# Attention in blocks of two steps: scores of both, then the other TensorE work, then values of both, with PSUM shared out for it

## The chip, the cores and the metric

The kernel runs on one core of one Trainium2 chip. The metric is the device time of one execution in microseconds. Before the change it is 6248.07 us, the median of three runs (6247.93 to 6248.6).

## The reference, cut to what matters

The input is x, four images of 128 channels and 64 by 64 points, all in float32. Layer 0 is softmax attention over the 4096 points of an image, with four heads of 32 channels:

```python
attn = jax.nn.softmax(jnp.einsum('bhnd,bhmd->bhnm', Q, K) * scale, axis=-1)
out = jnp.einsum('bhnm,bhmd->bhnd', attn, V)
...
y = out @ Wo + bo + x_flat          # then a layer norm over the channels
```

Layer 1 adds three things computed from the output of layer 0: a 3x3 convolution, a mixing of channels in the frequency plane (in the kernel two Hilbert and channel matmuls and a flipped addition), and a selective scan ("mamba") along the 4096 points:

```python
xs = silu(conv1d(xi));  dt = softplus(dt_proj(x_dbl))
h  = exp(dt * A) * h + dt * B * xs  # 256 channels x 16 states
y  = (C . h + xs * D) * silu(z);  ym = y @ out_proj
return spatial + spectral + ym
```

## The kernel before, in words

**Units of work.** The 4096 points of an image are cut into chunks of 512 (32 chunks in all). A *half* H is one chunk of queries with one pair of heads; there are 64. A half takes 32 *steps*, one for each tile of 128 keys, so there are 2048 steps. The main loop (lines 984 to 1023) counts steps with `t`; one pass of it writes the instructions of one step[...].

**One step of attention.** `scores_for_exp` (line 470) computes the scores of 128 keys against 512 queries for two heads: six matmuls (query, low part of the query, minus the maximum), each on 64 of the 128 rows of TensorE, into two PSUM banks; ScalarE turns them into `e = exp(s)` in SBUF (line 486). `scores_for_max` (line 422) computes scores for the half that comes next: four matmuls of the same 64-row kind, whose maximum VectorE takes (line 441, the tile `part`). `times_values` (line 489) multiplies e with the values: two matmuls with 33 output columns each, into PSUM tile `po`, which a whole half accumulates. The values of a step are written one step later, behind the scores of the next. So TensorE does: scores of t, values of t-1, scores of t+1, values of t, and so on. At the end of a half, ScalarE and VectorE copy `po` to `oz` (lines 507 and 508).

**All other work is in jobs.** Projections, transposes, the convolution, the gates and so on are generators (`project_q`, `maxima`, `sigmoid`, `convolve`, ...). A job yields a string of letters that says what it needs next: P a place for a TensorE piece, A for ScalarE, D for VectorE, B a PSUM bank. `Plan.step` (line 122) is called once in a step, after the scores and ahead of the values, and goes over the jobs by rank and due time (`plan.at`, lines 955 to 981). While attention runs, odd steps offer two places each of P, A and D; even steps offer one place of A only. So other TensorE work comes at most once in two steps, between scores and values.

**The scan.** Each chunk has two halves of the channels with 16 states each, so 32 *states* `v`. One state takes `scan_decay` (ScalarE, `dA = exp(dt*A)` into PSUM, line 780), `scan_input_term` (GpSimd, `db`, line 785) and `scan_state` (VectorE scan, line 793; GpSimd times C and sum, lines 796 to 812). One state is done in two steps. The scan of chunk c starts `LAG` = 2 x 64 + 16 steps behind the attention of chunk c, so when attention has ended, 144 steps of scan are left. In the last two chunks the sum over states is done on TensorE (line 806).

**PSUM.** [...] `s1` (two, scores for the maximum), `s2` (two, scores for exp), `o` (one, values), `dA` (one), `m0` and `m1` (one each, for all the jobs, given out by the plan and released some steps later).

Of the kernel before, what the change touches and what calls it, by code (L numbers as in the profile page):

```python
# [9 lines left out]
F32 = mybir.dt.float32  # L10
# [71 lines left out]
class Job:  # L82
# [4 lines left out]
    def __init__(self, gen):  # L87
        self.gen = gen
        self.done = False
        self.need = None  # L90
        self.advance(None)

    def advance(self, bank):
        try:
            self.need = self.gen.send(bank)
        except StopIteration:
            self.done = True


class Plan:  # L100


    def __init__(self, banks, buffers):
        self.t = None
        self.places = buffers
        self.seq = 0
        self.later = []
        self.jobs = []
        self.free = list(range(banks))
        self.freed = []  # L110

    def at(self, t, rank, gen):
        self.seq += 1
        self.later.append((t, rank, self.seq, gen))

    def now(self, rank, gen):
        self.at(self.t, rank, gen)

    def release(self, bank, steps=1):
        self.freed.append((self.t + steps, bank))  # L120

    def step(self, t, places):

        self.t = t
        self.places |= places
        self.free += [bank for when, bank in self.freed if when <= t]
        self.freed = [e for e in self.freed if e[0] > t]
        for e in sorted((e for e in self.later if e[0] <= t), key=lambda e: e[:3]):
            self.jobs.append((e[1], e[0], e[2], Job(e[3])))
            self.later.remove(e)  # L130
        self.jobs = sorted((j for j in self.jobs if not j[3].done), key=lambda j: j[:3])
        kept = 0
        for *_, job in self.jobs:
            bank = None
            if "B" in job.need and len(self.free) <= kept:
                continue
            if any(c != "B" and not self.places[c] for c in job.need):
                kept += "B" in job.need
                continue
            for c in job.need:  # L140
                if c == "B":
                    bank = self.free.pop(0)
                else:
                    self.places[c] -= 1
            job.advance(bank)
            while not job.done and job.need == "P" and self.places["P"]:
                self.places["P"] -= 1
                job.advance(None)
        self.jobs = [j for j in self.jobs if not j[3].done]

# [5 lines left out]
def attention_then_conv_mamba(  # L156
# [114 lines left out]
    def constants_of_attention():  # L271
        yield ""
# [3 lines left out]
    def constants_of_the_rest():  # L276


        yield ""
# [11 lines left out]
        yield ""  # L291
# [4 lines left out]
        yield ""  # L296
        nc.vector.tensor_scalar(negA, negA, -1.0, None, ALU.mult)


        bank = yield "PB"  # L300
        pb = bank_tile(bank, [P, 1], "pb")
        for k in range(PAIRS):
            nc.tensor.matmul(pb, Wo[k], bvk[:, k : k + 1], start=k == 0, stop=k == PAIRS - 1)
        yield "D"
        plan.release(bank, 2)
# [19 lines left out]
    plan = Plan(2, {"x": 2, "f": 1})  # L325

    def bank_tile(bank, shape, name):
        return psum.tile(shape, F32, tag=f"m{bank}", name=name)
# [10 lines left out]
    def project_kv(b, i):  # L339
# [5 lines left out]
        yield ""  # L345
        bank = yield "PB"
        pk = bank_tile(bank, [P, L], f"pk_{nm}")
        nc.tensor.matmul(pk, Wk, xk, start=True, stop=True)
        yield "DA"
        plan.release(bank, 2)  # L350
        hi = att.tile([P, L], F32R, tag="khi", name=f"khi_{nm}")
        lo = att.tile([P, L], F32R, tag="klo", name=f"klo_{nm}")
        nc.scalar.activation(hi, pk, AF.Identity, bias=bk)
        nc.vector.scalar_tensor_tensor(lo, pk, bk, hi, ALU.add, ALU.subtract)
# [4 lines left out]
        bank = yield "PB"  # L359
        pv = bank_tile(bank, [P, TPC, HEADS, HD], f"pv_{nm}")  # L360
# [8 lines left out]
        plan.places["x"] += 1  # L369
        yield "A"  # L370
        plan.release(bank)
        vst = att.tile([P, TPC, HEADS, HD + 1], F32, tag="vst", name=f"vst_{nm}", bufs=1)
# [30 lines left out]
    def project_q(H):  # L403
# [4 lines left out]
        bank = yield "PB"  # L408
        pq = bank_tile(bank, [P, L], f"pq_{H}")
        nc.tensor.matmul(pq, Wq[k], xqs[c], start=True, stop=True)  # L410
        yield "DA"
        plan.release(bank, 2)
        q = att.tile([P, 2, L], F32R, tag="Q", name=f"Q_{H}", bufs=3)
        bias = bq[:, k : k + 1]
        nc.scalar.activation(q[:, 1, :], pq, AF.Identity, bias=bias)
        nc.vector.scalar_tensor_tensor(q[:, 0, :], pq, bias, q[:, 1, :], ALU.add, ALU.subtract)
# [5 lines left out]
    def scores_for_max(H, s):  # L422
# [6 lines left out]

        tag = "s2" if H == 0 and s % 2 else "s1"  # L430
# [12 lines left out]
    def maxima(H):  # L443

        bank = yield "B"
# [8 lines left out]
        yield ""  # L454
        pm = bank_tile(bank, [P, L], f"pm_{H}")
# [4 lines left out]
        yield ""  # L460
        plan.release(bank, 2)
        mhi = att.tile([P, L], F32R, tag="th", name=f"mhi_{H}", bufs=1)
        mm = att.tile([P, L], F32R, tag="MX", name=f"MX_{H}")
        nc.scalar.activation(mhi, pm, AF.Copy, scale=-1.0)
        nc.vector.scalar_tensor_tensor(mm, mhi, minus_lo, pm, ALU.mult, ALU.subtract)
# [4 lines left out]
    def scores_for_exp(H, m):  # L470
# [4 lines left out]
        s = psum.tile([P, 2, L], F32, tag="s2", name=f"s2_{H}_{m}")  # L475
# [9 lines left out]
        e = att.tile([P, 2, L], F32, tag="e", name=f"e_{H}_{m}", bufs=3)  # L485
# [24 lines left out]
    def normalise(H, t0):  # L510
# [10 lines left out]
        yield ""  # L521
# [8 lines left out]
        yield ""  # L530
        nc.gpsimd.tensor_tensor(oz[k], oz[k], r, ALU.mult)  # L531
        if k == PAIRS - 1:
            plan.at(t0, 0, output_projection(H // PAIRS))
# [7 lines left out]
    def output_projection(c):  # L541
# [5 lines left out]
        bank = yield "PB"  # L547
        py = bank_tile(bank, [P, TPC, P], f"py_{c}")
        for t in range(TPC):
            if t == TPC // 2:  # L550
                yield "P"
            ts = slice(t * P, (t + 1) * P)
            for k in range(PAIRS):
                nc.tensor.matmul(py[:, t, :], oz[k][:, ts], Wo[k], start=k == 0, stop=False)  # L554
            nc.tensor.matmul(py[:, t, :], xr[:, ts], ident, start=False, stop=True)
# [5 lines left out]
        for t in range(TPC):  # L561
            nc.vector.bn_stats(st[:, t, :], py[:, t, :])
# [6 lines left out]
        yield ""  # L569
        nc.scalar.activation(q, v, AF.Ln)  # L570
        nc.scalar.activation(r, q, AF.Exp, scale=-0.5)
        yield ""
# [5 lines left out]
        yield ""  # L578
        yield "D"
        plan.release(bank, 2)  # L580

        xh = loc.tile([P, TPC, P], F32, tag="xh", name=f"xh_{c}", bufs=2)
        XH[c] = xh
        for t in range(TPC):
            nc.vector.tensor_scalar(
                xh[:, t, :],
                py[:, t, :],
# [9 lines left out]
    def sigmoid(z, tag, nm):  # L597
# [6 lines left out]
        bank = yield "AB"  # L604
        ln = bank_tile(bank, [P, L], f"ln_{nm}")
        nc.scalar.activation(ln, a, AF.Ln, bias=ones)
        yield "D"
        plan.release(bank, 2)
# [10 lines left out]
    def mamba_input(c):  # L619
# [14 lines left out]
        bank = yield "PB"  # L634
        pt = bank_tile(bank, [P, TPC, P], f"pt_{c}")
        for t in range(TPC):
            nc.tensor.transpose(pt[:, t, :], XH[c][:, t, :], ident)
        yield "A"
        plan.release(bank)
# [19 lines left out]
    def scan_input(c, hf):  # L659

        bank = yield "PB"
        pi = bank_tile(bank, [P, RPC, W], f"pi_{c}_{hf}")
        nc.tensor.matmul(pi, inw[:, hf * P : (hf + 1) * P], inner(c), start=True, stop=True)  # L663
        yield "A"
        plan.release(bank)
        xi = loc.tile([P, L + TAPS - 1], F32, tag=f"sg{hf}", name=f"xi_{c}_{hf}", bufs=1)
        nc.scalar.activation(xi[:, : TAPS - 1], carry[:, hf, :], AF.Copy)
        nc.scalar.activation(xi[:, TAPS - 1 :], pi.rearrange("p r w -> p (r w)"), AF.Identity)
        nc.scalar.activation(carry[:, hf, :], xi[:, L:], AF.Copy)
        s = loc.tile([P, L], F32, tag=f"xs{hf}", name=f"xs_{c}_{hf}", bufs=1)  # L670
        bank = yield "DB"
        ps = bank_tile(bank, [P, L], f"conv_{c}_{hf}")
# [13 lines left out]
        plan.release(bank, 2)  # L686
# [7 lines left out]
    def scan_bc(c):  # L694

        bank = yield "PB"
        pd = bank_tile(bank, [DTR + 2 * NS, L], f"pd_{c}")
        for hf in range(NH):
            nc.tensor.matmul(pd, xpw[:, hf, :], xss[c][hf], start=hf == 0, stop=hf == NH - 1)  # L699
        yield "A"  # L700
        plan.release(bank)
# [8 lines left out]
    def scan_dt(c, hf, xd):  # L710
        bank = yield "PB"
        pdt = bank_tile(bank, [P, L], f"pdt_{c}_{hf}")
# [5 lines left out]
        yield "A"  # L718
        plan.release(bank)
# [11 lines left out]
        bank = yield "AB"  # L731
        ln = bank_tile(bank, [P, L], f"lnw_{c}_{hf}")
        nc.scalar.activation(ln, w, AF.Ln)
        yield "DA"
        plan.release(bank, 2)
# [364 lines left out]
```

## Time and profile before

| | |
|---|---|
| median of three runs | 6248.07 us |
| the profiled execution: its own time | 6247.33 us |
| its span, first to last instruction | 6245.5 us |
| matmul rows on TensorE | 32076, busy 6001.6 us (96%) |
| busy: VectorE, ScalarE, GpSimd | 4284.2 us (69%), 3582.9 us (57%), 4605.3 us (74%) |
| first and last exp of the attention (line 486) | start at 130.7 and 5967.6 us |
| last scan of a state (line 793) | starts at 6230.6 us |
| granted TensorE clock, mean | 0.978 |

A float32 matmul appears as two rows (two passes). Rows of matmuls that run side by side on different parts of the array start a few ns apart. Their ends are modelled, and so this document works with the distance from one start to the next. In the timeline the columns are start, length, engine, line, operation, output <- inputs, shape and count, and in square brackets the idle time ahead of it and what ended it. Neighbouring equal rows are merged, "x4" being four of them; then the length runs from the first start to the last end.

### The profile page before, as it was taken

How to read it: one execution, taken by the hardware profiler on the slowest of the kernel's cores; microseconds unless marked ns; L12 is line 12 of the kernel's file. 1: busy time of each engine (PE TensorE's matmuls, PEld its weight loads, DVE VectorE, ACT ScalarE, POOL GpSimd, SP SyncE). 2: the span in 40 equal slices, each digit the busy share in tenths (PEclk: the TensorE clock that was granted, in tenths of full speed). 3: DMA queues.
4: the chain of work that ended last, by engine and by line, in shares of the span. 5: the costliest groups of instructions: out<-in, count | busy, mean ns of one | idle time of the engine just before them, and what ended most of it. 6: DMA issues, size and time to landing. Idle time of an engine off the chain costs nothing.

```text
span 6245.5 us, 83489 instructions
## 1 busy us (share of the span) xinstructions
PE 6001.6 (96%) x32076; PEld 2540.6 (41%) x32076; DVE 4284.2 (69%) x4405; ACT 3582.9 (57%) x4858; POOL 4605.3 (74%) x4951
## 2 busy tenths in 40 slices
PE   5999999999999999999999999999999999999956
PEld 2444444444444444444444444444444444444321
DVE  4556777777777677777767777767776766677556
ACT  1455666665666656566665556656565655665642
POOL 0006887777888777888887788877788877778866
PEclk7999999999999999999999999999999999999976
DMA  3002222223222222223232222222322222212223
GB/s 111 14 15 60 62 58 58 65 65 103 72 75 58 62 62 63 59 65 84 76 87 62 65 62 65 55 60 70 98 70 63 57 52 56 56 53 55 59 68 93
DMA packets 234225, 404.98 MB, mean 65 GB/s; under 512 B 38872, under 2 KB 40416, under 8 KB 233824
## 3 DMA queue, kind: packets, MB, share of 16 engines
q1 hardware_dynamic: 229440, 397.75, 23.3%
q8 instruction: 251, 4.11, 0.3%
q10 hardware_dynamic: 4384, 1.89, 0.1%
q14 instruction: 150, 1.23, 0.1%
HBM read 350.54 MB, written 49.02 MB: 64 GB/s over the span
## 4 chain that ended last, share of the span: by engine, by line
PE 80%; POOL 9%; DVE 5%; ACT 3%; issue 2%; DMA 1%; ACTq 0%; SPq 0%; POOLq 0%; DVEq 0%
PE po L498 27%; PE s L478 25%; PE s L434 13%; PE pf L857 4%; POOL hs L797 3%; DVE part L441 2%; ACT e L486 2%; DVE hs L793 2%; POOL db L785 1%; PE pi L663 1%; PE pdt L713 1%; POOL acc L812 1%; PE pq L410 1%; PE pd L699 1%; PE py L554 1%
## 5 line engine op out<-in xcount | busy, mean ns | idle before, releaser
L441 DVE TENSOR_REDUCE part<-s 128x2 f32<-128x1024 f32 x2048 | 2501.0, 1222 | 1613.6 <-PE s L434 1611.9
L486 ACT ACTIVATE e<-s 128x1024 f32<-128x1024 f32 x2048 | 2094.1, 1023 | 2257.5 <-PE s L478 2249.3
L498 PE MATMUL po<-e,V 128*33 128x512 f32 x8192 | 2160.1, 605 | 2.8 <-DVE oz L508 0.3
L478 PE MATMUL s<-Q,K 64*128 64x512 f32 x8192 | 1500.7, 444 | 25.3 <-ACT e L486 20.2
L793 DVE TENSOR_TENSOR_SCAN hs<-dA,state,db 128x512 f32<-128x512 f32 x1024 | 1305.7, 1275 | 158.9 <-ACT dA L780 69.2
L797 POOL TENSOR_TENSOR hs<-hs,bc 128x512 f32<-128x512 f32 x1024 | 1307.0, 1276 | 82.0
L434 PE MATMUL s<-K,Q 64*128 64x512 f32 x8192 | 1297.7, 395 | 44.4 <-DVE part L441 42.0
L478 PEld LDWEIGHTS s<-Q,K 64*128 64x128 f32 x8192 | 611.5, 185 | 1753.7 <-ACT e L486 1186.1
L785 POOL TENSOR_TENSOR db<-u,bc 128x512 f32<-128x512 f32 x954 | 1223.0, 1282 | 1.6 <-DMA bc<-bcd 1.6
L812 POOL TENSOR_TENSOR acc<-acc,hs 128x512 f32<-128x512 f32 x900 | 1151.7, 1280 | 70.6
L796 POOL COPY state<-hs 128x1 f32<-128x1 f32 x1024 | 212.6, 208 | 976.6 <-DVE hs L793 976.1
L434 PEld LDWEIGHTS s<-K,Q 64*128 64x128 f32 x8192 | 763.7, 186 | 280.5 <-DVE part L441 102.9
L478 PE MATMUL s<-MX,sel 64*128 64x512 f32 x4096 | 810.3, 392 | 0.0
L780 ACT ACTIVATE dA<-dt,negA 128x512 f32<-128x512 f32 x1024 | 702.5, 686 | 146.8 <-DVE hs L793 146.7
L498 PEld LDWEIGHTS po<-e,V 128*33 128x33 f32 x8192 | 299.2, 109 | 899.0 <-issue 865.0
L478 PEld LDWEIGHTS s<-MX,sel 64*128 64x128 f32 x4096 | 383.8, 184 | 90.0
L857 PE MATMUL pf<-xp,cw 128*128 128x512 f32 x576 | 288.2, 617 | 0.0
L450 POOL COPY wide<-mx 128x128 f32<-128x128 f32 x256 | 63.2, 292 | 196.9 <-DVE mx L447 196.9
L806 PE MATMUL acc<-hs,cst 128*128 128x512 f32 x128 | 110.8, 969 | 86.7 <-POOL hs L797 86.7
L531 POOL TENSOR_TENSOR oz<-oz,rz 128x512 f32<-128x512 f32 x64 | 81.9, 1279 | 106.7 <-DMA rz<-rd 106.7
L857 PEld LDWEIGHTS pf<-xp,cw 128*128 128x128 f32 x576 | 96.1, 188 | 131.9 <-issue 126.9
L554 PE MATMUL py<-wat_vo,oz 128*128 128x128 f32 x512 | 83.0, 285 | 22.6 <-POOL oz L531 18.6
(134 smaller groups left out, 3561.0 us busy)
## 6 DMA issues: line engine op xcount, KB each, us to landing
bc<-bcd SPq DMA_DIRECT2D x512, 512.0 KB
K<-kd SPq DMA_DIRECT2D x64, 256.0 KB
rz<-rd SPq DMA_DIRECT2D x128, 128.0 KB
vd<-vst SPq DMA_DIRECT2D x32, 264.0 KB
V<-vd SPq DMA_DIRECT2D x32, 264.0 KB
xq<-in_x SPq DMA_DIRECT2D x32, 256.0 KB
xk<-in_x SPq DMA_DIRECT2D x32, 256.0 KB
kd<-khi SPq DMA_DIRECT2D x32, 256.0 KB
```

The source lines that it names most:

```text
L434: nc.tensor.matmul(sc[:, j, :], QT[H][rows[j], n, t * P : (t + 1) * P], KK[k][m][rows[j], :], start=n == 0, stop=n == 1,)
L441: nc.vector.tensor_reduce(part[H][:, t, :, m], sc, AX.X, ALU.max)
L478: nc.tensor.matmul(s[:, j, :], sel[rows[j], :] if n == 2 else KK[k][i][rows[j], t * P : (t + 1) * P], mov[rows[j], :], start=n == 0, stop= ...
L486: nc.scalar.activation(e, s, AF.Exp)
L498: nc.tensor.matmul(po[H][used[j], :], VA[i][:, t, 2 * k + j, :], e[:, j, :], start=m == 0, stop=m == NT - 1,)
L780: nc.scalar.activation(dA[c, v], dts[c][hf], AF.Exp, scale=negA[:, k : k + 1])
L785: engine.tensor_tensor(db[c, v], us[c][hf], bcs[c, n][:, 0, :], ALU.mult)
L793: nc.vector.tensor_tensor_scan(hs, dA.pop((c, v)), db.pop((c, v)), state[:, k : k + 1], ALU.mult, ALU.add)
L796: nc.gpsimd.tensor_copy(state[:, k : k + 1], hs[:, L - 1 :])
L797: nc.gpsimd.tensor_tensor(hs, hs, bcs[c, n][:, 1, :], ALU.mult)
L812: nc.gpsimd.tensor_tensor(accs[c, hf], accs[c, hf], hs, ALU.add)
L857: nc.tensor.matmul(pf, cw[:, k, :], xps[c][:, dy : dy + RPC, dx : dx + W], start=k == 0, stop=False)
```

## The change

The loop now counts *blocks* `u` of two steps (a half has UH = 16, a chunk SLOT = 32 blocks, attention UNITS = 1024). TensorE's order in a block is: scores for the maximum of step 2u, scores for exp of 2u and of 2u+1, scores for the maximum of 2u+1, the jobs' work, values of 2u and of 2u+1. The values no longer lag by a step.

PSUM: `sA` (two banks) takes both scores for the maximum; `sB` (two banks) takes the scores for exp of 2u and then, in the same block, the jobs' temporary tiles (T); `sC` (two banks) takes the scores for exp of 2u+1 and then dA; `m` (one bank, need M) takes the sums that last over blocks (convolution and conv1d); `o` is as before. A job that takes a temporary tile must evacuate it in the same block: its need names all at once (`PTA`: matmul, tile and ScalarE place), and the VectorE operations that read such a tile are in a phase of their own ("g", need G), written after the scan of the block. D-jobs come in a first phase between the two maxima. `bn` now reads a copy in SBUF that ScalarE makes; the output projection is done in two parts in two blocks; the convolution does one matmul (C) in a block. The places in a block are P 2, C 1, T 2, A 3, D 2, E 1, G 1. LAG becomes 64 blocks (128 steps), LEAD 8 steps, e has two buffers in place of three, and bc is loaded for state pair n+2, at even v.

```diff
-    def step(self, t, places):
...
+    def begin(self, u, places):
+        self.u = u
+        self.places = dict(places)
+        self.temps = []
+        self.buffers["M"] += sum(when <= u for when in self.freed)
+        self.freed = [when for when in self.freed if when > u]
+
+    def phase(self, kinds):
...
         for *_, job in self.jobs:
...
+            while not job.done and self.may(job, kinds):
+                bank = None
+                for c in job.need:
+                    if c == "T":
+                        if not self.temps:
+                            self.temps = self.temporary(u)
+                        bank = self.temps.pop(0)
+                    elif c == "M":
+                        bank = self.lasting(u)
+                    if c in self.buffers:
+                        self.buffers[c] -= 1
+                    elif c != "g":
+                        self.places[c] -= 1
+                job.advance(bank, u)
         self.jobs = [j for j in self.jobs if not j[3].done]
+
+    def may(self, job, kinds):
+        if not job.need:
+            return "" in kinds and self.u > job.u
+        if any(c not in kinds for c in job.need):
+            return False
+        left = self.places | self.buffers | {"g": 9}
+        return all(left[c] >= job.need.count(c) for c in job.need)
...
-    def bank_tile(bank, shape, name):
-        return psum.tile(shape, F32, tag=f"m{bank}", name=name)
+    def temporary(u):
+
+        t = psum.tile([P, 2, L], F32, tag="sB", name=f"tmp_{u}")
+        return [t[:, 0, :], t[:, 1, :]]
+
+    def lasting(u):
+        return psum.tile([P, L], F32, tag="m", name=f"sum_{u}")
...
@@ def project_q(H):
-        bank = yield "PB"
-        pq = bank_tile(bank, [P, L], f"pq_{H}")
+        pq = yield "PTAG"
         nc.tensor.matmul(pq, Wq[k], xqs[c], start=True, stop=True)
-        yield "DA"
-        plan.release(bank, 2)
...
         nc.scalar.activation(q[:, 1, :], pq, AF.Identity, bias=bias)
+        yield "g"
         nc.vector.scalar_tensor_tensor(q[:, 0, :], pq, bias, q[:, 1, :], ALU.add, ALU.subtract)
...
@@ def sigmoid(z, tag, nm):
         nc.scalar.activation(a, a, AF.Exp, scale=-1.0)
-        bank = yield "AB"
-        ln = bank_tile(bank, [P, L], f"ln_{nm}")
+        ln = yield "ATG"
         nc.scalar.activation(ln, a, AF.Ln, bias=ones)
-        yield "D"
-        plan.release(bank, 2)
+        yield "g"
         nc.vector.scalar_tensor_tensor(a, z, 0.0, ln, ALU.min, ALU.subtract)
...
@@ def scores_for_exp(H, m, tag):
-        e = att.tile([P, 2, L], F32, tag="e", name=f"e_{H}_{m}", bufs=3)
+        e = att.tile([P, 2, L], F32, tag="e", name=f"e_{H}_{m}", bufs=2)
...
@@ def output_projection(c):
+        xh = loc.tile([P, TPC, P], F32, tag="xh", name=f"xh_{c}", bufs=2)
+        for t0 in range(0, TPC, 2):
+            bank = yield "PPTA"
+            py = bank[:, : 2 * P].rearrange("p (t c) -> p t c", t=2)
...
+            nc.scalar.activation(xh[:, t0 : t0 + 2, :], py, AF.Identity)
...
@@ def scan_decay(c, v):
-        tag = "o" if plan.t >= HALVES * NT + 2 and v % 2 else "dA"
-        dA[c, v] = psum.tile([P, L], F32, tag=tag, name=f"dA_{c}_{k}")
+        if plan.u > UNITS and v % 2:
+            dA[c, v] = psum.tile([P, L], F32, tag="o", name=f"dA_{c}_{k}")
+        else:
+            dA[c, v] = psum.tile([P, 2, L], F32, tag="sC", name=f"dA_{c}_{k}")[:, 0, :]
...
@@ def convolve(c):
         for k in range(9):
             if k:
-                yield "P"
+                yield "PC"
...
+    def maxima_of(t):
+        h, s = divmod(t + LEAD, NT)
+        if 0 <= h + 1 < HALVES:
+
+            scores_for_max(h + 1, s, "sC" if h < 0 and s % 2 else "sA")
+
+    places = {"P": 2, "C": 1, "T": 2, "A": 3, "D": 2, "E": 1, "G": 1}
+    most = {"P": 4, "C": 4, "T": 2, "A": 4, "D": 4, "E": 4, "G": 4}
+    u = 3 - SLOT
     end = (CHUNKS + 3) * SLOT
...
+    while u < end or not plan.idle():
+        busy = -LEAD // 2 <= u < UNITS
+        plan.begin(u, places if busy else most)
+        H, m = divmod(2 * u, NT)
+        v = u - LAG
+        scan = 0 <= v < CHUNKS * STATES
+        maxima_of(2 * u)
+        plan.phase(["D", "M"])
         if 0 <= H < HALVES:
+            scores_for_exp(H, m, "sB")
+            scores_for_exp(H, m + 1, "sC")
+        maxima_of(2 * u + 1)
+        if scan:
+            scan_decay(*divmod(v, STATES))
+
+        n = v // NH + 2
+        if v % NH == 0 and 0 <= n < CHUNKS * NS:
+            scan_load(*divmod(n, NS))
+        plan.phase(["P", "C", "T", "A", "E", "G", "M", "x", "f", ""])
+        if scan:
+            scan_state(*divmod(v, STATES))
+        if 0 <= v + 2 < CHUNKS * STATES:
+            late = u > UNITS
+            scan_input_term(*divmod(v + 2, STATES), nc.vector if late else nc.gpsimd)
+        plan.phase(["g"])
+        if 0 <= H < HALVES:
             times_values(H, m)
+            times_values(H, m + 1)
+        u += 1
```

Jobs are handled alike throughout: the other projections (`project_kv`, `scan_input`, `scan_bc`, `scan_dt`, `gate`, `spectral`, `mamba_input`) trade `PB` ... `A`/`D` for `PTA` or `PPTA`, and `scan_dt` takes its logarithm with `AATG`. The due times of the jobs are halved, from steps to blocks, some with small shifts (the gates at block 5 of a chunk, mamba input at 8, the convolution at 19).

## The prediction

> **What bounds the kernel now.** I read the busy shares first, then the chain of work that ended last, then the costliest groups.
>
> ```profile
> PE 6001.6 (96%) x32076; PEld 2540.6 (41%) x32076; DVE 4284.2 (69%) x4405; ACT 3582.9 (57%) x4858; POOL 4605.3 (74%) x4951
> PE 80%; POOL 9%; DVE 5%; ACT 3%; issue 2%; DMA 1%; ACTq 0%; SPq 0%; POOLq 0%; DVEq 0%
> L441 DVE TENSOR_REDUCE part<-s 128x2 f32<-128x1024 f32 x2048 | 2501.0, 1222 | 1613.6 <-PE s L434 1611.9
> L609 DVE SCALAR_TENSOR_TENSOR sg_x<-xs,ln_x 128x512 f32<-128x512 f32 x64 | 43.3, 676 | 3.1 <-ACT ln_x L606 3.1
> PE s L434 <- DVE part L441: 42.0, 81, 1.3
> PE s L478 <- ACT e L486: 20.2, 25, 1.5
> ```
>
> TensorE is on 80% of the chain, and VectorE and ScalarE mostly idle for TensorE's scores. TensorE itself waits for them only 42.0 + 20.2 us. But 96% is modelled; how full it is shows in the distances between starts. One step without other work, in the timeline of all engines around 5420 us:
>
> ```profile
> 5419.60 0.73 PE L478 MATMUL s<-Q,K 64*128 64x512 f32 x4
> 5420.18 0.39 PE L478 MATMUL s<-MX,sel 64*128 64x512 f32 x2
> 5420.41 0.62 PE L434 MATMUL s<-K,Q 64*128 64x512 f32 x4
> 5420.67 1.02 ACT L486 ACTIVATE e<-s 128x1024 f32<-128x1024 f32 x1 [0.80 <-PE s L478]
> 5420.95 1.05 PE L498 MATMUL po<-e,V 128*33 128x512 f32 x4
> 5421.07 1.23 DVE L441 TENSOR_REDUCE part<-s 128x2 f32<-128x1024 f32 x1
> 5421.59 0.69 ACT L780 ACTIVATE dA<-dt,negA 128x512 f32<-128x512 f32 x1
> 5421.94 0.73 PE L478 MATMUL s<-Q,K 64*128 64x512 f32 x4
> 5422.20 1.11 ACT L733 ACTIVATE lnw<-u 128x512 f32<-128x512 f32 x2
> ```
>
> Rows run in pairs (two heads side by side). The MX pair takes 5420.41 - 5420.18 = 0.23. The first two pairs take 0.58, so the first takes 0.35, which is 0.12 too much. The two K,Q pairs take 0.54 up to the first value, 0.08 more than 0.46. The values (two passes) take 0.99. A pass of 512 columns takes 0.43, from the timeline of the tail, where 16 of them run without a break, (7.03 - 0.59)/15:
>
> ```profile
> 6049.77 7.03 PE L857 MATMUL pf<-xp,cw 128*128 128x512 f32 x16
> ```
>
> So 0.13 of the 0.99 is not work. **Each round of scores and values loses 0.12 + 0.08 + 0.13 = 0.33 us** in a step of 2.34. What a real wait looks like, in the timeline at 532 us:
>
> ```profile
> 530.98 1.22 DVE L441 TENSOR_REDUCE part<-s 128x2 f32<-128x1024 f32 x1
> ...
> 532.25 0.73 PE L434 MATMUL s<-K,Q 64*128 64x512 f32 x4
> ...
> 532.92 0.15 PEld L498 LDWEIGHTS po<-e,V 128*33 128x33 f32 x4 [0.37 <-issue]
> ```
>
> The reduction ends at 532.20, TensorE goes on 0.05 later, and its two pairs then take 0.67 instead of 0.54: a wait costs its length plus some 0.12.
>
> [...]
>
> **The change, part by part** (1024 blocks; times from the block's start on TensorE).
>
> *One round less.* Today a block of two steps has two rounds, with or without jobs between them; then it has one: -0.33 x 1024 = **-338 us**. A block without jobs falls from 4.68 to 4.35. The jobs' matmuls stay; by the planner's rules I count 21 of 32 blocks per chunk with TensorE jobs, and the trace before has 20.7 (613 of 949 pairs of steps from 500 to 5960 us), so this is nothing.
>
> *Both maxima in sA.* The first one's second pair starts at 0.35; VectorE begins 0.43 later (5420.64 to 5421.07), takes 1.23, and release takes 0.05: free at 2.06. TensorE arrives after six exp pairs, 0.35 + 7 x 0.23 = 1.96. It waits 0.10 and reloads for 0.12, in every block: **+225 us**. Bounds: 0.10 (loads slip ahead of the wait, +102) to 0.35 (VectorE 0.13 late, +358). Behind the waiting matmuls stand the whole of the jobs and the values. Today s1 has a full step, and the same release is free.
>
> *Values in the same block.* The last pair of the first exp scores starts at 1.04, its e at +0.49 = 1.53 (5420.18 to 5420.67), until 2.55. Without jobs the values arrive at 2.06 + 0.35 + 0.23 + 0.08 = 2.72: no wait. The second e starts 2.45 (ScalarE starts the next some 0.10 before the end: 5421.59 against 5421.69), ends 3.47; its values come at 2.72 + 0.89 = 3.61. **0**, and covered by 0.1 us only. Two buffers of e suffice for the same reason.
>
> *Jobs' tiles in sB, read by VectorE behind the scan.* In a block with one 512-column job TensorE needs 0.12 + 0.86 + 0.10 more, and everybody is done in time. The exposed ones are logarithms in blocks without TensorE work. From the due times and places, these are blocks 6 and 10 of a chunk (gate) and 15 and 17 (scan input). ScalarE there: second e 2.45, dA 3.37, jobs from 3.98 (dA to lnw 0.61). In 15, 17 abs, exp, ln are 0.62 + 0.62 + 0.68: 5.90; in 6 xr (0.61), exp and ln give the same; in 10 exp and ln 5.28, but the scan (dA ends 4.06, + 0.05 + 1.27) holds VectorE until 5.38. Then 0.68 (row L609) and twice 0.05 of release: sB free at 6.68, 6.68, 6.68 and 6.11. TensorE wants it for the next exp at 4.57 + 0.58 = 5.15. With the reload: 1.65 three times and 1.08, less 0.22 each, since the next sA wait vanishes behind it: 5.2 us per chunk. For 31 chunks of scan input and 30 of gates **+157 us** (bounds: 0, if other matmuls fall into these blocks, to 300, if pq, pm and lnw are exposed as well).
>
> *End of a half.* oz on ScalarE, then VectorE (0.59 + 0.69, rows L507, L508) now stand ahead of the next maximum: 0.4 on average x 64 = **+26** (0 to 45).
>
> *Today's waits* (62 us, with 106 reloads of 0.12) belong to the order that goes: **-75** (0 to -90).
>
> *Small.* Output projection in two parts, [...] its ScalarE copies (some 0.45 each, half of a 128x512 row) lie beside 1.3 us of TensorE work; bn and xh push the second reduction, +3. DMAs: bc, loaded later by its place, waits for the same GpSimd product as today and still has two blocks; zd, zc and rd keep their distance on SP: 0.
>
> *Tail.* LAG leaves 64 states behind the attention instead of 72. The first ones there take 3.17 each, GpSimd bound:
>
> ```profile
> 5984.19 1.28 DVE L793 TENSOR_TENSOR_SCAN hs<-dA,state,db 128x512 f32<-128x512 f32 x1 [3.37 <-POOL acc L812]
> 5987.36 1.28 DVE L793 TENSOR_TENSOR_SCAN hs<-dA,state,db 128x512 f32<-128x512 f32 x1 [1.16 <-POOL acc L812]
> ```
>
> 8 x 3.2 = 26, and a little for jobs put ahead of the sum on TensorE: **-28** (0, if the last chunk's own chain sets the end, to -45).
>
> Sum: -338 + 225 + 157 + 26 - 75 + 10 - 28 = -23. From the profiled execution's 6247.3 that is 6224; the median of the runs is 0.7 higher: **6225 us**. The gain is real and mostly handed back at PSUM.
>
> **Rivals.** (1) *Forecast*: most comes back through sA and sB; own range 6150 to 6300. Chance 0.45. (2) *sB is covered*: the logarithms fall beside matmuls or the scan is early; the 157 go: 6225 - 157 = 6068, say 6070. For it: 21 of 32 blocks have cover. Against: A 3 and rank leave those four blocks to ScalarE alone. Chance 0.20. (3) *VectorE becomes the bound, slower.* Place: a block without jobs. Its second reduction starts at 2.41 + 0.43 = 2.84, ends 4.07; the scan waits for dA, 4.11 to 5.38; the next first reduction is due at 4.57 + 0.78 = 5.35. The slack is nil where today the scan has a bank of its own and nobody on TensorE behind it. From there each delay of the scan (db from GpSimd, busy 74%; a job's operation ahead of it) goes straight into sA, and beyond 0.4 into sC too. If the scan is 0.5 late in the 11 blocks without jobs of each of 30 chunks: +165, so 6390. Against: GpSimd prepares db two states ahead. Chance 0.35. That the rounds don't fall to one is excluded by the order in which the loop writes.
>
> **Numbers.** 0.2% (12.5 us) is about what a measurement of this kernel can tell from no change. Faster: all of (2) and just over half of (1), 0.45. Same: 0.10. Slower: (3) and the rest of (1), 0.45. The range takes in the middle of (2) and of (3): 6075 to 6390, leaving a tenth on each side.
>
> **What would show it.** Right: score runs of ten pairs with one change per block; in each block TensorE idle before L434 for VectorE (part) by 0.1, about 1000 times; idle before exp scores for VectorE (sg_x, sg_z) by 1 to 1.6, about 120 times; a tail some 28 us shorter. Wrong: the first wait is absent or far over 0.1; sB waits also for Q, MX and dt, or for none; TensorE idle for scan tiles in sC. A result under 6100 refutes the sB term, one over 6350 the claim that VectorE keeps up.

## The result, and the profile after

The changed kernel takes **6486.22 us** (median of four runs, 6482.18 to 6490.97), the kernel before 6248.00 beside it. The ratio is 1.038, with a 95% interval from 1.036 to 1.040: 238 us slower. The forecast was 6225, and its range ended at 6390. The profiled execution took 6482.18 us with a span of 6480.4, against 6224 forecast for it: 258 us are to be explained.

First the busy shares and the chain of work that ended last, after the change:

```profile
PE 5923.2 (91%) x32076; PEld 2624.0 (40%) x32076; DVE 4457.2 (69%) x4396; ACT 3688.8 (57%) x4922; POOL 4632.6 (71%) x4960
...
PE 65%; ACT 14%; DVE 9%; POOL 4%; issue 4%; DMA 3%; SPq 0%; ACTq 0%; POOLq 0%; DVEq 0%
```

TensorE has the same 32076 rows, but its share of the chain falls from 80% to 65%, and ScalarE rises from 3% to 14%. VectorE, which the third rival feared, rises only to 9%. TensorE's waits (line, releaser, total us, times, longest) say for whom it stands still:

```profile
PE s L444 <- DVE part L451: 95.9, 143, 1.5
PE s L486 <- DVE sg_x L611: 92.3, 62, 2.4
...
PE s L486 <- DVE sg_z L611: 71.6, 60, 1.5
PE tmp L663 <- ACT mhi L471: 39.1, 31, 1.4
PE tmp L813 <- ACT xi L666: 29.3, 31, 1.1
PE tmp L746 <- ACT Q L426: 27.1, 29, 1.0
PE tmp L423 <- ACT vst L388: 19.6, 24, 0.8
```

The rows of sg_x and sg_z were forecast: the scores for exp wait in sB for the logarithms of two gates, 163.9 us. (The waits behind the forecast's 157 come to some 170 without their reloads.) The last four were not: matmuls of jobs wait for ScalarE, once per chunk each. Nor were most of the first row's 95.9 us: 37.4 stand in block 11 of the chunks, where VectorE is late by `xh`, 25.9 in block 0 and 10.5 in block 16, which follow the end of a half. The short wait that was forecast for the second maximum of every block hardly shows here; its place is the waits of the weight loads, because there the load is the instruction that waits:

```profile
PEld s L444 <- DVE part L451: 811.4, 1356, 2.3
```

These 811 us are idle time of the loads, mostly behind matmuls that still run, so they are no cost. The cost is read from the distance of starts, in a block without jobs:

```profile
2018.79 0.74 PE L444 MATMUL s<-K,Q 64*128 64x512 f32 x4
...
2020.29 0.19 PEld L486 LDWEIGHTS s<-MX,sel 64*128 64x128 f32 x2
...
2020.52 0.40 PE L486 MATMUL s<-MX,sel 64*128 64x512 f32 x2
2020.86 0.30 PEld L444 LDWEIGHTS s<-K,Q 64*128 64x128 f32 x4 [0.38 <-DVE part L451]
2020.86 0.73 PE L444 MATMUL s<-K,Q 64*128 64x512 f32 x4
...
2021.52 1.91 PE L506 MATMUL po<-e,V 128*33 128x512 f32 x8
...
2023.36 0.73 PE L444 MATMUL s<-K,Q 64*128 64x512 f32 x4
```

The second maximum follows its last MX pair by 0.34 where an unhindered pair follows by 0.23. Behind this wait the load starts with its matmul, both at 2020.86, while the MX pair's started 0.23 ahead of it (2020.29); and the values follow by 0.66 instead of 0.54, which is the forecast's reload of 0.12. The block takes 4.57 us: just the forecast. A block with one 512-column job (26 of a chunk) takes 5.61, where the forecast's terms give 4.57 + 0.12 + 0.86 + 0.10 = 5.65. So such a job costs 1.04, of which its two passes of 0.43 are 0.86, and 0.18 come on top. The surprise is in blocks with two temporary tiles. Block 5 of a chunk, with the matmuls of `pq` (L423) and `pz` (L746):

```profile
2040.56 1.94 ACT L494 ACTIVATE e<-s 128x1024 f32<-128x1024 f32 x2 [1.96 <-PE s L486]
...
2041.82 1.12 PE L423 MATMUL tmp<-xq,wq_t 128*128 128x512 f32 x2
...
2042.54 0.69 ACT L771 ACTIVATE dA<-dt,negA 128x512 f32<-128x512 f32 x1
...
2043.16 0.67 ACT L426 ACTIVATE Q<-tmp,bq 128x512 fp32r<-128x512 f32 x1
...
2043.88 0.30 PEld L746 LDWEIGHTS tmp<-xp,inw 128*128 128x128 f32 x2 [1.77 <-ACT Q L426]
2043.88 1.13 PE L746 MATMUL tmp<-xp,inw 128*128 128x512 f32 x2 [0.94 <-ACT Q L426]
...
2044.94 0.15 PEld L506 LDWEIGHTS po<-e,V 128*33 128x33 f32 x4 [0.76 <-issue]
```

The first job's two passes start at 2041.82. The second job's start only 0.05 after ScalarE has finished reading the first tile (2043.16 + 0.67 = 2043.83), although it writes the other bank. In the trace this job's weight load (1.77) and its first pass (0.94) both wait for ScalarE's semaphore, so it is the program's own order that holds them, and it goes by the tile and not by the bank. ScalarE comes late: the second e, until 2042.50, and dA, from 2042.54, stand ahead of Q. So TensorE idles 0.94 us with the values behind it.

Lengths of some blocks, from e to e two steps on (us, medians over 16 chunks), and of a chunk (median of those chunks). Jobs lie in other blocks in other kernels, so a gain is read from the last column; blocks 5 and 22 of after and matmuls_first do hold the same TensorE jobs:

| kernel | block 1 (no job) | 5 | 13 | 14 | 22 | chunk |
|---|---|---|---|---|---|---|
| before | 4.75 | 7.35 | 5.70 | 4.67 | 5.79 | 183 |
| after | 4.56 | 7.69 | 7.61 | 7.72 | 7.60 | 192.6 |
| matmuls_first | 4.58 | 6.49 | 6.06 | 6.38 | 6.50 | 185 |
| one_temporary | 4.57 | 5.76 | 5.75 | 5.46 | 6.50 | 188 |

### The profile page after: what moved, and what is told of

Read it like the earlier page. It is cut to its first block, busy times and chain, and to the rows that moved or that the text cites. A ratio compares the mean times of both kernels' runs of the same rounds, so it can differ in the third digit from the quotient of the medians.

```text
span 6480.4 us, 84221 instructions
## 1 busy us (share of the span) xinstructions
PE 5923.2 (91%) x32076; PEld 2624.0 (40%) x32076; DVE 4457.2 (69%) x4396; ACT 3688.8 (57%) x4922; POOL 4632.6 (71%) x4960
## 4 chain that ended last, share of the span: by engine, by line
PE 65%; ACT 14%; DVE 9%; POOL 4%; issue 4%; DMA 3%; SPq 0%; ACTq 0%; POOLq 0%; DVEq 0%
PE po L506 21%; PE s L486 15%; PE s L444 15%; ACT e L494 7%; DVE part L451 4%; PE sum L840 4%; ACT dA L771 3%; POOL hs L788 2%; DMA xk<-in_x 2%; DVE hs L784 2%; DVE xh L589 1%; PE tmp L562 1%; PE tmp L707 1%; ACT tmp L609 1%; PE tmp L894 1%
## 5 line engine op out<-in xcount | busy, mean ns | idle before, releaser
L494 ACT ACTIVATE e<-s 128x1024 f32<-128x1024 f32 x2048 | 1986.9, 1022 | 2217.2 <-PE s L486 2217.2
L506 PE MATMUL po<-e,V 128*33 128x512 f32 x8192 | 1986.6, 599 | 1.4 <-ACT e L494 1.2
L444 PE MATMUL s<-K,Q 64*128 64x512 f32 x8192 | 1501.0, 445 | 101.7 <-DVE part L451 95.9
L486 PE MATMUL s<-Q,K 64*128 64x512 f32 x8192 | 1302.1, 395 | 171.8 <-DVE sg_x L611 92.3
L444 PEld LDWEIGHTS s<-K,Q 64*128 64x128 f32 x8192 | 621.5, 186 | 1320.1 <-DVE part L451 811.4
L486 PEld LDWEIGHTS s<-Q,K 64*128 64x128 f32 x8192 | 750.8, 184 | 428.4 <-DVE sg_x L611 113.6
L506 PEld LDWEIGHTS po<-e,V 128*33 128x33 f32 x8192 | 389.4, 109 | 1194.4 <-issue 594.3
L840 PE MATMUL sum<-xp,cw 128*128 128x512 f32 x576 | 318.6, 638 | 0.0
L685 POOL TENSOR_TENSOR xs<-xs,sg_x 128x512 f32<-128x512 f32 x64 | 82.1, 1282 | 111.2 <-ACT sg_x L613 111.2
L840 PEld LDWEIGHTS sum<-xp,cw 128*128 128x128 f32 x576 | 91.9, 192 | 129.7 <-issue 129.7
```

The costliest lines, as they stand in the source:

```text
L444: nc.tensor.matmul(sc[:, j, :], QT[H][rows[j], n, t * P : (t + 1) * P], KK[k][m][rows[j], :], start=n == 0, stop=n == 1,)
L486: nc.tensor.matmul(s[:, j, :], sel[rows[j], :] if n == 2 else KK[k][i][rows[j], t * P : (t + 1) * P], mov[rows[j], :], start=n == 0, stop= ...
L494: nc.scalar.activation(e, s, AF.Exp)
L506: nc.tensor.matmul(po[H][used[j], :], VA[i][:, t, 2 * k + j, :], e[:, j, :], start=m == 0, stop=m == NT - 1,)
L840: nc.tensor.matmul(pf, cw[:, k, :], xps[c][:, dy : dy + RPC, dx : dx + W], start=k == 0, stop=False)
```

## Experiments

Every kernel was timed beside the kernel before, whose median there was 6249.1 to 6250.8. Unless said otherwise the base is the changed kernel, 6486.

**matmuls_first.** A free need "h" splits each job behind its matmuls:

```diff
         nc.tensor.matmul(pq, Wq[k], xqs[c], start=True, stop=True)
+        yield "h"
         q = att.tile([P, 2, L], F32R, tag="Q", name=f"Q_{H}", bufs=3)
...
+        plan.phase(["h"])
+        plan.phase(["C", "T", "A", "G", "M", "x", "f", ""])
```

> The changed kernel, but in each block all matmuls of the jobs are written first, and the copies by ScalarE that read the temporary tiles after the last of them. Theory (two temporary tiles of one block are halves of one PSUM tile, and TensorE waits at the second until ScalarE has read the first): the waits for mhi, xi, Q and vst (115 us in the trace of the changed kernel) and their weight reloads go, blocks 5, 13, 14 and 22 of a chunk fall from 7.6-7.7 to about 6.5 us: -115 to -150 us, so about 6350. Rival (VectorE is the bound, TensorE's waits only take up its slack): within 30 us of 6486.

Measured: 6293.65, ratio 1.0068 (1.0053 to 1.0083), 193 us less. Block 5 again:

```profile
1987.55 1.12 PE L425 MATMUL tmp<-xq,wq_t 128*128 128x512 f32 x2
...
1988.52 1.02 PE L755 MATMUL tmp<-xp,inw 128*128 128x512 f32 x2
...
1989.47 0.15 PEld L510 LDWEIGHTS po<-e,V 128*33 128x33 f32 x4 [0.76 <-issue]
1989.47 1.91 PE L510 MATMUL po<-e,V 128*33 128x512 f32 x8
1989.58 0.69 ACT L429 ACTIVATE Q<-tmp,bq 128x512 fp32r<-128x512 f32 x1 [0.61 <-PE tmp L755]
```

From the first job to the values there are now 1.92 us in place of 3.12, and ScalarE's copies lie beside the values. Now it is ScalarE that waits 0.61 us for the second job's matmul, although it reads only the first job's half of the tile. All four of TensorE's waits are gone. VectorE's work is unchanged, so the rival falls. The gain is 43 us over the expected bound, and some jobs also came to lie in other blocks. Blocks 5 and 22, whose TensorE jobs are the same in both kernels, fall by 1.20 and 1.10, some 0.27 more than their waits of 0.93 and 0.82. By that the 115 waits are worth about 115 + 115 x 0.27 = 146 us (an estimate), which leaves 47 for the moved jobs.

**one_temporary.** The other way to have no second tile:

```diff
-    places = {"P": 2, "C": 1, "T": 2, "A": 3, "D": 2, "E": 1, "G": 1}
+    places = {"P": 2, "C": 1, "T": 1, "A": 3, "D": 2, "E": 1, "G": 1}
```

> The changed kernel, with one temporary tile per block in place of two; ScalarE's copies stay directly behind their matmuls. Theory (it is the second tile of a block that waits for ScalarE): without second tiles these waits go (115 us and some 15 for reloads)[...]: -60 to -170, so about 6380. Rival (matmuls_first gained because some jobs landed in other blocks, or because ScalarE's other work came earlier): within 30 us of 6486.

Measured: 6367.78, ratio 1.0196 (1.0181 to 1.0212), 118 us less, within the expected range, which had an estimate of 28 us in it for TensorE jobs in blocks of their own. The four waits are gone here too, while TensorE's jobs take 23 blocks of a chunk instead of 21. So two different edits that end the wait at the second tile recover 193 and 118 of the 238 us; both also move jobs.

**half_max.** For the wait at the second maximum:

```diff
-        nc.vector.tensor_reduce(part[H][:, t, :, m], sc, AX.X, ALU.max)
+        part_of = sc[:, :, : L // 2] if s % 2 == 0 else sc
+        nc.vector.tensor_reduce(part[H][:, t, :, m], part_of, AX.X, ALU.max)
```

> The changed kernel, but the maximum of every even step is taken over half of the keys only (so half of the queries subtract a smaller number before exp); the matmuls stay. VectorE's first reduction of a block takes 0.65 us instead of 1.23. Theory (each block waits 0.10 us at the second maximum and reloads weights for 0.12): blocks without jobs fall from 4.57 to 4.35, most others by 0.22: -180 to -225 us, so about 6280. Rival (VectorE is the bound in most blocks): -300 us or more, as VectorE saves 0.58 in each of 1024 blocks. Third (only the waits that the trace shows as TensorE idle count, not the reload): -95 us.

Measured: 6414.21, ratio 1.0260 (1.0243 to 1.0277), 72 us less. VectorE was relieved of 502 us (4457.2 to 3954.9 busy), so it is not the bound, and the rival falls. The theory's size falls too: a block without jobs shrinks by 0.12 and not by 0.22. The total is nearest to the third view, which counted idle time alone, but by luck: 1024 x 0.12 would be 123 us. The trace's granted TensorE clock shows where most of the difference can have gone. During the attention half_max has 35 stretches at half clock, 119.5 us in all, where the changed kernel has one of 3.4 (the last section shows one of them). At half speed they take back at most (119.5 - 3.4)/2 = 58 us, and 72 + 58 = 130; even that is far from the rival's 300. The timeline shows what is late next:

```profile
2001.56 0.39 PE L487 MATMUL s<-MX,sel 64*128 64x512 f32 x2
...
2001.79 0.62 PE L444 MATMUL s<-K,Q 64*128 64x512 f32 x4
...
2002.38 1.97 PE L507 MATMUL po<-e,V 128*33 128x512 f32 x8
...
2003.29 0.15 PEld L507 LDWEIGHTS po<-e,V 128*33 128x33 f32 x4 [0.77 <-ACT e L495]
```

The second maximum now follows at once (0.23). But the values of the second step wait for the second e: they start 0.91 after the first ones instead of 0.86. Where jobs follow, their blocks have other limits.

**ln_in_sbuf.** The logarithm no longer holds sB; every job keeps its block:

```diff
-        ln = yield "ATG"
+        yield "AG"
+        ln = loc.tile([P, L], F32, tag="ln", name=f"ln_{nm}", bufs=1)
```

> The changed kernel, but the logarithm of sigmoid goes to a tile in SBUF instead of a temporary tile in sB. Theory (scores for exp wait for VectorE's sg_x and sg_z through sB, 164 us of TensorE idle in the trace): these waits go; -130 to -165 us, so about 6335. Rival (the waits would reappear at the next maximum, since VectorE is as late for sA as for sB): -0 to -40 us.

Measured: 6696.19, ratio 1.071 (1.069 to 1.073), 210 us *more*, and neither view holds. One chunk around block 16:

```profile
2170.99 1.28 POOL L789 TENSOR_TENSOR hs<-hs,bc 128x512 f32<-128x512 f32 x1
2171.03 1.78 DVE L612 SCALAR_TENSOR_TENSOR sg_x<-xs,ln_x 128x512 f32<-128x512 f32 x1 [0.38 <-ACT ln_x L610]
...
2172.84 0.69 DVE L516 COPY oz<-po 33x512 f32<-33x512 f32 x1
...
2173.57 1.23 DVE L451 TENSOR_REDUCE part<-s 128x2 f32<-128x1024 f32 x1
...
2174.85 0.89 PE L444 MATMUL s<-K,Q 64*128 64x512 f32 x4 [3.18 <-DVE part L451]
```

VectorE's instruction takes 1.78 us instead of 0.69: GpSimd's of 1.28 began 0.04 earlier, VectorE's ends 0.54 after it, and then everything behind it is late for sA. This goes with the operand: over the run sg_x takes 1.73 on average with both inputs in SBUF. With one in PSUM, in the changed kernel, each of the 64 took 0.69, though 61 of them ran beside a GpSimd instruction of over 0.5 us. The expectation had missed it. Part of the 210 is the clock: 65 stretches of the attention, 252.6 us, are at half clock, which costs at most 125 us more than in the changed kernel. So this run doesn't test sB.

**ln_in_m**, on matmuls_first (6294): the logarithm stays in PSUM, in bank m.

```diff
-        ln = yield "ATG"
+        ln = yield "AMG"
...
         nc.vector.scalar_tensor_tensor(a, z, 0.0, ln, ALU.min, ALU.subtract)
+        plan.release()
```

> The kernel of matmuls_first, but the logarithm of sigmoid is put in the PSUM bank m (that of the convolution's sums) instead of a temporary tile in sB; VectorE reads PSUM as before, and some jobs move by a block or two. Theory (scores for exp wait for sg_x and sg_z through sB: 129 us of TensorE idle in the trace of matmuls_first and some 90 weight reloads of 0.12): -100 to -140 us on 6294, so about 6170, which would be faster than the kernel before. Rival (VectorE is as late for the first maximum as for sB): 0 to -30 us, and TensorE's wait moves to the maximum's scores.

Measured: 6316.63, ratio 1.0108 (1.0093 to 1.0123), 23 us more, and neither view holds. The waits at sB are gone, and block 9 falls from 6.47 to 4.57. But block 10 rises from 5.05 to 7.90, where the four `xh` instructions (0.33 each in the changed kernel where no such GpSimd instruction runs) take 3.35 us beside two of GpSimd's:

```profile
2019.74 1.27 POOL L814 TENSOR_TENSOR acc<-acc,hs 128x512 f32<-128x512 f32 x1
2020.45 3.35 DVE L594 TENSOR_SCALAR xh<-xh,mv,r 128x128 f32<-128x128 f32 x4
...
2020.96 1.28 POOL L787 TENSOR_TENSOR db<-u,bc 128x512 f32<-128x512 f32 x1
...
2023.73 1.21 DVE L454 TENSOR_REDUCE part<-s 128x2 f32<-128x1024 f32 x1
...
2024.99 0.73 PE L447 MATMUL s<-K,Q 64*128 64x512 f32 x4 [1.82 <-DVE part L454]
```

**xh_gpsimd** (on the changed kernel), **first_xh** (on matmuls_first) and **ln_in_m_xh_gpsimd** (on ln_in_m) take that operation off VectorE:

```diff
-        yield "D"
         XH[c] = xh
         for t in range(TPC):
-            nc.vector.tensor_scalar(
+            nc.gpsimd.tensor_scalar(
```

> The changed kernel, but the layer norm's last step (xh minus mean, times r, four instructions per chunk) is done by GpSimd instead of VectorE. On VectorE two of the four take 1.3 to 1.4 us instead of 0.33, while a GpSimd instruction of 1.28 us runs. Theory ([...] the delay of 2 us goes through the first maximum into TensorE's order): block 11 or 12 of each chunk falls by 0.5 to 1 us: -15 to -35 us, so about 6460. Rival (hidden): within 8 us of 6486.

> The kernel of matmuls_first, with xh's normalisation on GpSimd; the logarithms stay in sB. It tells which of the two edits of ln_in_m_xh_gpsimd brought it from 6294 to 6259. Theory A (the sB waits cost what TensorE's idle time says[...]): 6275 to 6295. Theory B ([...] without the sB wait VectorE is just as late for sA): 6250 to 6262.

> The kernel of ln_in_m, with xh's normalisation on GpSimd as in xh_gpsimd. Theory (the two gains add, 9 us having been measured for the second): 5 to 30 us below ln_in_m. Rival (the gain came from jobs' places[...]): no difference beyond 8 us.

Measured: 6477.19 (ratio 1.0364, 1.0348 to 1.0379), 9 us less, which the intervals don't tell from nothing; 6323.37 (1.0119, 1.0105 to 1.0133), 30 us more; 6258.91 (1.0014, 1.0008 to 1.0021), 58 us less. So the same edit is worth -9, +30 and -58 us on three bases, and no run isolates the price of `xh`'s delay beside GpSimd. Two things differ between the bases: the blocks in which `xh` and the jobs behind it fall, and the clock. Time at half clock during the attention is 47.8 us in matmuls_first, 102.4 in first_xh, 78.5 in ln_in_m and 20.5 in ln_in_m_xh_gpsimd. Half of each difference is the most that it can cost: 27 of the 30 us more, 29 of the 58 less. The last two of the three kernels differ only in where the logarithm lies (and the jobs that follow it): 64 us is the measured price of sB, up to 41 of it by the clock. Theory A of first_xh, with this delay as the rest, and theory B, with this delay as the whole, both fall. TensorE's waits in first_xh,

```profile
PE s L490 <- DVE sg_x L615: 85.0, 62, 2.4
PE s L447 <- DVE part L454: 58.8, 88, 1.5
PE s L490 <- DVE sg_z L615: 48.5, 30, 1.6
```

and in ln_in_m_xh_gpsimd:

```profile
PE s L447 <- DVE part L454: 134.2, 194, 1.5
```

Of 133.5 us of waits that go, 75.4 come back at the maximum: VectorE was late for it as well, and the wait ahead of it had hidden this.

**values_lag**, on matmuls_first: the second round of a block put back (`place_v`, which puts the values of an image in place, also comes a block later).

```diff
             scores_for_exp(H, m, "sB")
+        if 0 < u <= UNITS:
+            times_values(*divmod(2 * u - 1, NT))
+        if 0 <= H < HALVES:
             scores_for_exp(H, m + 1, "sC")
...
             times_values(H, m)
-            times_values(H, m + 1)
```

> The kernel of matmuls_first, but the values of the odd step are written a block later, between the two exp scores, as the kernel before had them a step late; so each block has two rounds of scores and values again. Theory (a round costs 0.33 us, and the second maximum's wait for the first, worth 0.12 in a block without jobs by half_max and less in others, goes): blocks without jobs rise from 4.57 to about 4.78, all in all +60 to +340 us on matmuls_first's 6294 us, most likely +200. Rival (a round costs TensorE nothing that counts, only the waits do): -60 to 0 us.

Measured: 6775.54, ratio 1.0842 (1.0826 to 1.0858), 482 us more, above the expected range; more half clock (160.4 us against 47.8) is at most 56 of it. A block without jobs takes 5.10:

```profile
2129.84 1.05 PE L510 MATMUL po<-e,V 128*33 128x512 f32 x4
2129.95 1.23 DVE L454 TENSOR_REDUCE part<-s 128x2 f32<-128x1024 f32 x1 [1.59 <-PE s L447]
...
2131.24 0.73 PE L447 MATMUL s<-K,Q 64*128 64x512 f32 x4 [0.34 <-DVE part L454]
```

The wait in sA didn't go, as the expectation had it. It moved to the next block's first maximum, where it is 0.34. Without it the block is 4.76, against 4.45 in half_max, which has no such wait either: 0.31 for a round, 0.33 forecast. The rival falls.

**ln_in_m_xh_prologue** and **first_xh_prologue**: another tile for each early block.

```diff
-        t = psum.tile([P, 2, L], F32, tag="sB", name=f"tmp_{u}")
+        tag = "sB" if u >= -20 else ("sA", "sB", "sC")[u % 3]
+        t = psum.tile([P, 2, L], F32, tag=tag, name=f"tmp_{u}")
```

> The kernel of ln_in_m_xh_gpsimd, but before block -20, while the maxima do not yet use sA and sC, the temporary tiles go round sB, sA and sC. Theory (the 18 to 23 us that the time before the first exp has grown by come from the key and value projections of successive blocks waiting for one another in sB): 10 to 20 us below 6259, so about 6243, level with or just below the kernel before. Rival (the loads of x or the constants set the start): 0 to -4 us.

> The kernel of first_xh with the tiles of ln_in_m_xh_prologue before block -20. Expected: the same step from first_xh as ln_in_m_xh_prologue takes from ln_in_m_xh_gpsimd, 10 to 20 us by the theory, none by its rival.

Measured: 6261.42 (ratio 1.0019, 1.0011 to 1.0027) and 6317.98 (1.0110, 1.0096 to 1.0124), 2.5 more and 5.4 less than their bases. The theory falls: TensorE then waits for loads of x instead (21.6 us once).

**load_x_early**, on ln_in_m_xh_gpsimd, in whose trace the key projection waits for x during attention too:

```profile
2067.66 1.10 PE L365 MATMUL tmp<-xk,wk_t 128*128 128x512 f32 x2 [0.91 <-DMA xk<-in_x]
```

```diff
-        xk = load_x(b * NCH + i, "xk", 2)
+        xk = load_x(b * NCH + i, "xk", 3)
         yield ""
+        if b:
+            yield ""
...
-    plan = Plan(temporary, lasting, {"x": 2, "f": 1, "M": 1})
+    plan = Plan(temporary, lasting, {"x": 3, "f": 1, "M": 1})
```

> The kernel of ln_in_m_xh_gpsimd, with three buffers for xk in place of two and x loaded two blocks ahead of its key projection in place of one. Theory (in the trace the key projection of the next image waits 0.9 us for the load of x in its block, in some of 24 blocks, and the projections before the first exp wait for loads too): 5 to 25 us below 6259, so about 6245 and level with or just below the kernel before. Rival (the loads are covered by later waits): within 4 us of 6259.

Measured: **6242.90**, ratio 0.9989 (0.9983 to 0.9996), 16 us less than its base. The first exp starts at 141.2 instead of 153.8, and block 21 falls from 7.64 to 6.49. It is below the kernel before by 7 us, and the smallest of all.

## Why the prediction was wrong

**The step that failed** is "The jobs' matmuls stay; ... so this is nothing". I counted blocks with TensorE work (21 of 32, as before) and priced their matmuls, but not the new rule that the job's copy follows in the same block, out of one tile. The count holds (the trace after has 21 too); the price of nothing doesn't. In four blocks of a chunk two jobs now take TensorE, ScalarE, TensorE in turn. The trace shows 115 us of idle for it, worth some 146; undoing it gave 193 us, moved jobs included, or 118 with two more blocks of TensorE jobs in a chunk. The forecast asked of each bank when its users are done. It didn't ask which users share a *tile*: that TensorE waits, by a semaphore, for a reader of the tile's other bank is shown.

**One round less, and both maxima in sA** (-338 and +225): the net is right: a block without jobs was forecast to fall from 4.68 to 4.57 and is 4.57; values_lag gives 0.31 for a round. The +225 as a term of its own is too large: taking the wait away shortened a block without jobs by 0.12 of the 0.22, since the second e is then late, and the kernel by 72 us; the half clock is at most 58 of what is missing.

**Values in the same block: 0.** Right as long as the sA wait is there, and the cover of 0.1 named in the forecast is what half_max used up.

**Jobs' tiles in sB** (+157): the idle time came nearly as forecast (164 of some 170), and in its place it costs about what was priced: blocks 6, 10, 15 and 17 take 6.54 us more in a chunk than four free ones, some 200 us, less about 0.12 in each block behind them: 185 (an estimate). But removing it is worth only 64, the clock included, because VectorE is as late for the next maximum.

**End of a half** (+26): block 0, which follows one, takes 5.50, so 0.93 more than a block without jobs, where 0.4 was forecast. Over 31 chunks, with block 16, this comes to some 40 us (an estimate). But in block 0 it is not new. In the kernel before that block took 5.78, 1.03 more than block 1, and its trace has the copy of `oz` and the scan ahead of the maximum too:

```profile
2109.22 0.69 DVE L508 COPY oz<-po 33x512 f32<-33x512 f32 x1 [0.39 <-ACT oz L507]
...
2109.94 1.28 DVE L793 TENSOR_TENSOR_SCAN hs<-dA,state,db 128x512 f32<-128x512 f32 x1
...
2111.15 1.20 DVE L441 TENSOR_REDUCE part<-s 128x2 f32<-128x1024 f32 x1
...
2112.40 0.73 PE L434 MATMUL s<-K,Q 64*128 64x512 f32 x4 [0.48 <-DVE part L441]
```

So block 0 became 0.28 shorter, and this end of a half, priced as new, was one of today's waits.

**Today's waits** (-75): they went with their order, as forecast, but others came. TensorE's wait for the maximum, 42.0 us before, is 95.9 after; most of it stands in blocks 11, 0 and 16, as said above.

**Small** (+10: bn and xh at +3, and an estimate of +7 for the output projection in two blocks): the four `xh` instructions, 0.40 each before, now read SBUF, and two of them take 1.3 to 1.4 beside GpSimd instructions of 1.28. That was not in the forecast at all. Block 11 of a chunk, which has no TensorE job, takes 5.80 by it, some 36 us over 29 chunks; xh_gpsimd, which takes it away, moves jobs and gains 9.

**DMA 0, and the start:** the first exp is 17.8 us later (148.5 against 130.7). load_x_early removes 12.6 of such a delay on its base: two buffers of x, asked for once a block, are late at the start. I had looked only at bc and the zd chain.

**Tail** (-28): it is 273.5 us, and was 277.9, so -4. Engines in the tail of after and of before (busy us of TensorE, weight loads, VectorE, ScalarE, GpSimd):

```profile
6206.00:6481.00 275.00, 171.10 (x262) 55.97 (x262) 150.90 (x164) 79.30 (x129) 158.53 (x173) 0.68 0.32 79
```

```profile
5967.00:6246.00 279.00, 163.69 (x264) 54.07 (x260) 171.07 (x182) 86.83 (x145) 182.81 (x197) 0.67 0.33 84
```

GpSimd did save 24 us of work, but it is busy for 58% of the tail: the first states' rate, which I multiplied, isn't the tail's. What else sets its length was not tried.

**The balance.** From first to last exp the attention takes 6058.4 us after and 5836.9 before: 221.5 more, where the forecast's terms add up to +5. So 216.5 of the 258 us are missing there, 17.8 at the start and 23.6 in the tail. An estimate from the block lengths splits the 216.5: two-job blocks 146, block 11 36, sB 185 - 157 = 28, end of a half 40 - 26 = 14, together 224. This says where the time stands and not what removing a part would bring.

**The rival that VectorE becomes the bound** gave the nearest time, 6390, and I had written that over 6350 would refute that VectorE keeps up. This was a bad test, since other losses lead there too. half_max speaks against that rival: 502 us less VectorE work, 72 us gained, 130 at most without the half clock. VectorE is late in single blocks (0, 11, 16), not in all.

## What to carry to other kernels

When scratch tiles are cut from one larger buffer, list who writes and who reads it within one round, in the order of each queue. Two jobs in it cost a round trip between engines (here 0.94 us of idle in block 5), unless all the writers come first (then none). An idle time in the trace is not its price: here 115 us of it brought 193 or 118, and 133.5 brought 64. Ask who is late behind it, which jobs move, and what the clock does. And a forecast that ends at a total should not be tested by the total, but by the blocks.

## What the runs showed of the hardware

With an operand moved from PSUM to SBUF, VectorE's `sg_x` went from 0.69 to 1.73 us on average. `xh` took 0.39 to 0.41 from PSUM in the kernel before and takes 0.33 to 1.45 from SBUF in the changed one. Of its 128 instructions there, 65 overlap a GpSimd instruction of over 0.5 us; 61 of these take 1.29 to 1.45 and end 0.08 to 0.09 after GpSimd's. The 63 that overlap none take 0.33 to 0.34. Both delays reach TensorE by the next maximum. In ln_in_sbuf a lower clock followed TensorE's pause of 3.18 us, shown above. In three stretches around it, the granted clock (third value from the end) is

```profile
2168.00:2174.80 6.80, 3.66 (x24) 1.58 (x20) 6.36 (x7) 6.44 (x10) 3.92 (x4) 1.00 0.12 39
2174.80:2179.00 4.20, 4.15 (x8) 1.47 (x8) 3.79 (x4) 0.00 (x0) 1.82 (x4) 0.59 0.28 64
2179.00:2182.40 3.40, 3.40 (x22) 1.65 (x23) 0.73 (x1) 0.63 (x2) 3.32 (x3) 1.00 0.22 82
```

so TensorE came back at 0.59 for 4 us. In half_max the clock fell behind a pause half as long:

```profile
1895.63 0.74 PE L487 MATMUL s<-Q,K 64*128 64x512 f32 x4 [1.67 <-DVE sg_x L612]
```

```profile
1893.10:1896.40 3.30, 1.63 (x12) 0.97 (x12) 2.65 (x4) 2.20 (x4) 1.87 (x3) 1.00 0.00 0
1896.40:1899.80 3.40, 3.40 (x14) 1.88 (x11) 3.06 (x4) 2.80 (x4) 2.10 (x2) 0.50 0.51 146
1899.80:1903.20 3.40, 3.40 (x14) 0.94 (x14) 1.46 (x2) 1.09 (x2) 2.68 (x4) 1.00 0.21 67
```

A pause of 1.67 us filled half of one stretch of 3.3 us, and the next 3.4 us were granted at 0.50. Over the attention, the changed kernel has 3 pauses of 1.6 us or more and one stretch at half clock; half_max has 95 and 35, first_xh 60 and 30, ln_in_sbuf 116 and 65. Of the three, those of 1.66 and 2.42 us at 6102 and 6127 were followed by full clock, that of 2.42 at 6139 by the stretch. The 88 pauses of the changed kernel between 1.4 and 1.6 us lowered its clock nowhere. Not every stretch follows a pause: nine of the 13 stretches in load_x_early, and three of the four in the kernel before, follow within 3.4 us of the matmuls of `pdt`, which use 8 of the 128 rows, without a pause of 1.4 us. Whether these matmuls lower the clock, no run tested.
